# A piece of background work moved between the maxima and the sums of values in each attention step

## The chip, the cores and the metric

The kernel runs on one core of a Trainium2 chip. The metric is the device time of one execution, in microseconds (us); lower is better.

## The reference, cut to what matters

Two transformer layers with cross-attention act on x (2048 rows of 256 numbers, 16 heads of 16). Layer one splits x into two halves of 1024 rows: self-attention within each half, attention of each half to the other one, and an MLP with GELU. Layer two does self-attention under a mask that is given as integers (2048 x 2048), attention to a context of 1601 rows, and an MLP with ReLU.

```python
# layer one: x0, x1 are the two halves of x
x0 = x0 + g_msa[:, 0] * mha(mod(ln(x0)));  x1 = x1 + g_msa[:, 1] * mha(mod(ln(x1)))   # stage 0
ox = attend(qx, ky, vy) @ crs_proj_w;      oy = attend(qy, kx, vx) @ crs_proj_w       # stage 1
x  = x + g_mca * (ox, oy);  x = x + g_mlp * (gelu(z @ fc1 + b) @ fc2 + b)
# layer two
x = layernorm(x + mha(x, x, x, mask))          # stage 2, scores = where(mask == 0, -1e9, scores)
x = layernorm(x + mha(x, memory, memory))      # stage 3, memory: 1601 rows
x = layernorm(x + relu(x @ w1 + b1) @ w2 + b2)
```

## The kernel before, in words

The four attentions are four stages (0 to 3), and all of them run in one stream (`stream`). A **unit** is one block of 512 queries with one group of four heads. There are 16 units in each of the stages 0, 1 and 3, and 20 in stage 2, where one block's keys are taken in two parts. A unit has 16 steps in stages 0 and 1, 16 or 32 in stage 2, and 26 in stage 3: 1440 steps in all. A **step** handles one tile of 128 keys for two of the four heads. Stage 2 is the one with a mask (`masked`).

Each step puts up to four kinds of work on TensorE:

- **Scores** (`weights_of`, `second[s2]()` in `stream`): two matmuls at L938 and two at L945, which use 64 rows of the array each, so that two run side by side. With a mask two more at L953 add the bias, with the full 128 rows and 128 columns, in bf16. The result lies in a tile `s_ps` of two banks, and ScalarE's exponential (L958) takes it from there into `e`.
- **Maxima** of a later unit (`take_maxima`, L860), of the same 64-row shape, also into `s_ps`. VectorE reduces them, at L875, or at L868 with a mask. There are three tiles `s_ps`, and scores and maxima take them in turn. `todo` says at which step each is due. When all of a unit's maxima are there, VectorE negates and splits them (L885 to L891), and three steps later `as_rows` turns them into rows (L899); ScalarE copies these to `nm` (L904), which L945 of the next unit reads.
- **Sums of values** (`values_of`, L975): four matmuls side by side, each on 32 columns of the array. They run in two passes, so the trace has eight. They read `e` of tiles that are two steps old or older. Most steps have half a tile, 256 columns; the first and the last tile of a unit are taken whole, with an empty step after each.
- **Pieces** of background work: the projections, transposes and MLPs that turn the output of a stage into the input of the next. They are generators (`chain_self`, `chain_cross` and so on), and each of their matmul groups is a `piece`. A piece takes a PSUM bank, runs its matmuls, and yields; its last step is the **eviction**, which reads the bank. Lines: transposes L343 (eviction on ScalarE, L354 or L358), queries and keys L385 (ScalarE `hi` L392, then VectorE `lo` L393, then two stores), values L415 (VectorE L425), output projection L460 and the second half of the MLP L535 (VectorE L478 or L490), the first half of the MLP L515 (ScalarE L523). All matmuls of pieces use the full array and fp32, which runs in two passes.

While the stream runs, pieces use one of two single banks, `small[0]`. The other one holds the sums of values of the running unit, and the two change places after a unit's third step (`s2 == 2`). There ScalarE also copies the sums of the unit before out of its bank (`copy_sums`, L1007).

The order of instructions on every engine is the order in which the program issues them. In `stream` a step calls, in turn: `before()`, which evicts the piece of the step before; `take_maxima`; the sums of values and the scores (with a mask the scores first); and `after(step)`, which advances the counter `now`, does what is due in `later` (`as_rows`, reciprocals and divisions among it), makes mask columns (L828), issues one transfer (`load_ready`), and starts the next piece through `advance`. So the matmuls of a piece come after a step's last TensorE work, and its eviction comes first in the next step.

The MLP with GELU has a peculiarity: with `wait` set, its first half only adds the bias, and eight GELU activations (L534) run together in the first step of its second half (`down`), so that ScalarE's function table is changed once for the eight.

Of the kernel before, what the change touches and what calls it, by code (L numbers as in the profile page):

```python
# [66 lines left out]
def slot_rows(st, slot):  # L67
    return sum(key_rows(st, n) for n in KEYS[st][slot])


def slots_of(st, b):

    return ((b // 2,), (1 - b // 2,), (0, 1), (0, 1))[st]
# [3 lines left out]
def two_layers(ctx: ExitStack, tc: tile.TileContext, a: dict, out: bass.AP):  # L77
# [17 lines left out]

    small = [1]
    streaming = [False]
    unfinished: list = []

    def flush(banks):  # L100
# [93 lines left out]
    def hidden(shape, dtype=F32, name="hid"):  # L194
        return sb.tile(shape, dtype, tag="hidden", bufs=HB, name=name)
# [310 lines left out]
    def mlp(w, ci, func, hT, finish, between=None):  # L506
        w1, w2 = w
        hid: list = [None] * (DFF // P)


        wait = func != AF.Relu and streaming[0]

        def up(m, f):
            for k in range(2):
                nc.tensor.matmul(  # L515
                    m, lhsT=w1[k][:, f * P : (f + 1) * P], rhs=hT[:, k, :],
                    start=k == 0, stop=k == 1,
                )

        def take(m, f):  # L520
            hid[f] = hidden([P, BLK])
            bias = cols[:, ci + f : ci + f + 1]
            nc.scalar.activation(hid[f], m, AF.Identity if wait else func, bias=bias)  # L523

        for f in range(DFF // P):
            yield from piece(lambda m, f=f: up(m, f), lambda m, f=f: take(m, f))
        if between is not None:
            between()

        def down(m, n, q2):  # L530
            qt = 2 * n + q2
            for f in range(DFF // P):
                if wait and qt == 0:
                    nc.scalar.activation(hid[f], hid[f], func)  # L534
                nc.tensor.matmul(  # L535
                    m[:, q2 * D : (q2 + 1) * D], lhsT=hid[f][:, qt * P : (qt + 1) * P],
                    rhs=w2[f // 4][:, f % 4, :], start=f == 0, stop=f == DFF // P - 1,
                )

        for n in range(2):  # L540
            yield from piece(
                *(lambda m, n=n, q2=q2: down(m, n, q2) for q2 in range(2)),
                lambda m, n=n: finish(n, m.rearrange("p (t d) -> p t d", d=D)),
            )
# [555 lines left out]
    def stream(stages):  # L1100

        units = []
        for st in stages:
            for b in ORDER[st]:
                blocks[st, b] = {}
                if (st, b) == (2, SPLIT):
                    units += [
                        {"st": st, "b": b, "g": g, "slots": (slot,), "part": slot}
                        for slot in range(2) for g in range(NG)
                    ]  # L1110
                else:
                    units += [
                        {"st": st, "b": b, "g": g, "slots": slots_of(st, b)} for g in range(NG)
                    ]
        for i, u in enumerate(units):
            u["i"] = i

        columns: list = []
        at = 0
        for u in units:  # L1120
            steps = [(slot, kt) for slot in u["slots"] for kt in range(-(-slot_rows(u["st"], slot) // P))]
            if u["st"] == 2 and u["g"] == 0:
                columns += [
                    (at + 2 * n - COLUMNS, u["b"], slot, kt) for n, (slot, kt) in enumerate(steps)
                ]
            u["start"], u["steps"] = at, 2 * len(steps)
            at += 2 * len(steps)

        todo: list = []
        for u, w in zip(reversed(units), [*reversed(units[:-1]), None]):  # L1130
            tiles = maxima(u)
            n = len(tiles)
            begin, length = (w["start"], w["steps"]) if w else (-n, n)
            for k in range(n - 1, -1, -1):
                due = begin + k * length / n - AHEAD
                if u.get("part") == 1 and u["g"] == 0:

                    due = begin + (n - 1) * length / n - AHEAD - (n - 1 - k) * SPACING
                todo.append([min(due, todo[-1][0] - SPACING) if todo else due, u, tiles[k]])

        def take_maxima(step):
            while todo and todo[-1][0] <= step:
                _, u, f = todo.pop()
                f()
                if not todo or todo[-1][1] is not u:
                    all_maxima(u)

        def all_maxima(u):
            negated(u)
            later.append([3, lambda: as_rows(u), True])  # L1150
            if u.get("part") == 0 and u["g"] == NG - 1:
                want(2, 1, 1)

        def before():

            if unfinished and background and not background[0][2] and background[0][1] <= now[0]:
                if not advance(background[0]):
                    background.pop(0)

        def after(step):  # L1160

            now[0] += 1
            due = [x for x in later if x[0] <= 0]
            later[:] = [[x[0] - 1, *x[1:]] for x in later if x[0] > 0]
            for x in due:
                x[1]()
            turned = any(x[2] for x in due)
            while columns and columns[0][0] <= step:
                mask_columns(*columns.pop(0)[1:])
                turned = True  # L1170
            load_ready()
            soon = any(x[0] <= 0 and x[2] for x in later)
            soon = soon or (columns and columns[0][0] <= step + 1)
            if background and background[0][1] <= now[0]:
                if not background[0][2] or not (turned or soon):
                    if not advance(background[0]):
                        background.pop(0)

        streaming[0] = True
        for u in units[:2]:  # L1180
            load_queries(u)
        for step in range(math.floor(todo[-1][0]), 0):
            small[0] = 1
            before()
            take_maxima(step)
            after(step)
        pending: list = []
        step = 0
        for u in units:
            i = u["i"]  # L1190
            masked = u["st"] == 2
            small[0] = i % 2
            second = weights_of(u)
            for s2 in range(len(second)):
                before()
                if s2 == 3:
                    pending += values_of(u)
                if s2 == 1 and i + 2 < len(units):
                    load_queries(units[i + 2])
                take_maxima(step)  # L1200
                f = pending.pop(0) if pending else None
                if f and not masked:
                    f()
                second[s2]()

                if f and masked:
                    f()
                after(step)
                step += 1
                if s2 == 2:  # L1210
                    small[0] = (i + 1) % 2
                if s2 == 2 and i:
                    w = units[i - 1]
                    copy_sums(w)
                    part = w.get("part")
                    if part is None:
                        later.append([3, lambda w=w: invert(w), False])
                        later.append([6, lambda w=w: divide(w), False])
                    elif part == 1:
                        v = units[i - 1 - NG]  # L1220
                        later.append([3, lambda w=w, v=v: compare(w, v), False])
                        later.append([4, lambda w=w, v=v: invert_both(w, v), False])
                        later.append([7, lambda w=w: (fetch_first(w), divide(w)), False])
                    if w["g"] == NG - 1 and part != 0:
                        chain_after(w)
        small[0] = len(units) % 2
        for f in pending:
            if f:
                f()
        for x in later:  # L1230
            x[1]()
        flush((0, 1))
        streaming[0] = False
        w = units[-1]
        copy_sums(w)
        invert(w)
        divide(w)
        chain_after(w)
        while background:
            if not advance(background[0]):  # L1240
                background.pop(0)
        flush((None,))
# [92 lines left out]
```

## Time and profile before

| | us |
|---|---|
| median of 3 runs | 3392.64 |
| lowest and highest of them | 3391.25 and 3396.46 |
| profiled execution, its own time | 3403.53 |
| its span, first to last instruction | 3401.7 |
| TensorE matmuls busy | 3113.2 |
| VectorE busy | 2120.7 |
| ScalarE busy | 1713.7 |
| GpSimd busy | 404.6 |

The profiled execution has a time of its own, a little above the median. Numbers per instruction come from that one execution. The granted TensorE clock in it was 0.968 of full speed. From the first scores to the last, the four stages take 500, 639, 1237 and 815 us of the span; 131 us lie ahead of them and 79 us behind, counted from the start of one step's scores to that of another's.

In a line of the timeline the columns are the start, the duration, the engine, the line of the program, the operation, what it writes and reads, the shapes, and the number of instructions that are merged in the line; in square brackets stands the idle time ahead of it and what ended it. The ends of matmuls are modelled, so the distance between starts is the better measure on TensorE.

### The profile page before, as it was taken

The page shows a single profiled execution, that of the slowest core. Times are in us where ns is not written, and L with a number is a line of the kernel's source. Part 1 is how long each engine was busy: PE and PEld are TensorE (multiplying, and loading weights), DVE is VectorE, ACT ScalarE, POOL GpSimd, SP SyncE. Part 2 cuts the span into 40 slices and gives each one's busy share as a digit, 9 for nine tenths or more (in the row PEclk, how much of TensorE's full clock was granted, in tenths as well). Part 3 has the DMA queues.
Part 4 walks back from the last instruction along what each step waited for, and adds up shares of the span by engine and source line. Part 5 has one row for each costly group of instructions (what it writes and reads, how often), then busy time and mean ns, then how long its engine had stood idle before and what let it go on. Part 6 is the DMA issues. An engine that isn't in the chain of part 4 may idle for free.

```text
span 3401.7 us, 56761 instructions
## 1 busy us (share of the span) xinstructions
PE 3113.2 (92%) x22592; PEld 1362.0 (40%) x22592; DVE 2120.7 (62%) x3858; ACT 1713.7 (50%) x1868; POOL 404.6 (12%) x344
## 2 busy tenths in 40 slices
PE   4799999998999889898999999999999999999995
PEld 2334444444444433333333333343334444444433
DVE  2676766764646455366767777767656747657541
ACT  1265655655545445343555555554546646546461
POOL 0001101101010121104023012201010011110102
PEclk8799999999999999899999999999999999999997
DMA  5652162160204121343111001102241100000000
GB/s 177 140 105 65 36 117 65 48 128 24 65 18 114 32 84 37 94 100 107 51 39 51 15 20 58 32 17 55 49 87 43 26 10 26 25 18 26 10 14 16
DMA packets 162362, 191.20 MB, mean 56 GB/s; under 512 B 82584, under 2 KB 95520, under 8 KB 162096
## 3 DMA queue, kind: packets, MB, share of 16 engines
q1 hardware_dynamic: 162096, 187.57, 22.3%
q8 instruction: 178, 2.92, 0.4%
q14 instruction: 88, 0.72, 0.1%
HBM read 129.91 MB, written 48.46 MB: 52 GB/s over the span
## 4 chain that ended last, share of the span: by engine, by line
PE 51%; DVE 5%; ACT 4%; DMA 2%; SPq 2%; POOL 1%; issue 1%; ACTq 0%; POOLq 0%; DVEq 0%
PE m_ps L975 13%; PE s_ps L938 8%; PE s_ps L860 8%; PE s_ps L953 7%; PE s_ps L945 6%; ACT e L958 3%; PE m_ps L515 2%; DVE s_ps L868 2%; PE m_ps L535 2%; DVE pm L875 1%; PE m_ps L460 1%; DMA raw<-in_mask 1%; PE m_ps L385 1%; DVE t L328 1%; PE m_ps L415 1%
## 5 line engine op out<-in xcount | busy, mean ns | idle before, releaser
L958 ACT ACTIVATE e<-s_ps 128x1024 f32<-128x1024 f32 (+1 forms) x1440 | 1468.1, 1025 | 1375.0 <-PE s_ps L945 794.8
L875 DVE TENSOR_REDUCE pm<-s_ps 128x2 f32<-128x1024 f32 (+3 forms) x1024 | 1120.9, 1106 | 534.7 <-PE s_ps L860 530.2
L975 PE MATMUL m_ps<-e,V 128*32 128x256 f32 (+2 forms) x10432 | 903.6, 418 | 7.3 <-ACT hT L354 4.4
L868 DVE CUSTOM_DVE_ANT_0 s_ps<-s_ps,bias 128x512 f32<-128x512 f32 x1024 | 712.8, 701 | 295.4 <-PE s_ps L860 161.6
L860 PE MATMUL s_ps<-kT,q 64*128 64x512 f32 (+3 forms) x3072 | 676.6, 443 | 111.8 <-ACT e L958 51.1
L938 PE MATMUL s_ps<-q,kT 64*128 64x512 f32 (+1 forms) x2880 | 677.3, 466 | 51.8 <-ACT e L958 28.4
L945 PE MATMUL s_ps<-nm,sel 64*128 64x512 f32 (+1 forms) x2880 | 575.2, 395 | 0.1
L860 PEld LDWEIGHTS s_ps<-kT,q 64*128 64x128 f32 x3072 | 294.1, 186 | 528.1 <-issue 301.1
L938 PEld LDWEIGHTS s_ps<-q,kT 64*128 64x128 f32 (+1 forms) x2880 | 270.5, 184 | 496.6 <-issue 241.0
L975 PEld LDWEIGHTS m_ps<-e,V 128*32 128x32 f32 (+1 forms) x10432 | 206.9, 108 | 433.6 <-issue 415.3
L953 PE MATMUL s_ps<-biasT,ident 128*128 128x512 bf16 x1024 | 311.4, 386 | 0.0
L1053 POOL TENSOR_TENSOR oT<-oT,rd_rows 64x512 f32<-64x512 f32 x64 | 81.7, 1277 | 1904.8 <-DMA rd_rows<-rd_dr 1491.1
L945 PEld LDWEIGHTS s_ps<-nm,sel 64*128 64x128 f32 (+1 forms) x2880 | 275.2, 187 | 12.1 <-ACT nm L904 0.8
L805 POOL TENSOR_SCALAR bias<-raw 128x512 bf16<-128x512 int32 x64 | 123.1, 1924 | 266.4 <-DMA raw<-in_mask 256.4
L868 DVE DVE_READ_ACCUMULATOR2_ANT pm<- 128x1 f32 x1024 | 144.9, 141 | 0.0
L953 PEld LDWEIGHTS <-ident 128*128 128x128 bf16 x1024 | 58.4, 97 | 187.8 <-issue 187.8
L393 DVE SCALAR_TENSOR_TENSOR lo<-m_ps,qkb,hi 128x512 fp32r<-128x512 f32 (+2 forms) x56 | 41.1, 734 | 137.3 <-ACT hi L392 94.3
L535 PE MATMUL m_ps<-w_mlp,hid 128*128 128x256 f32 x448 | 111.4, 405 | 11.9 <-ACT hid L534 11.9
L385 PE MATMUL m_ps<-hT,w_qk 128*128 128x512 f32 (+2 forms) x224 | 109.8, 613 | 9.3 <-DVE lo L393 8.8
L515 PE MATMUL m_ps<-hT,w_mlp 128*128 128x512 f32 x224 | 111.0, 618 | 1.1 <-ACT hT L354 1.1
L535 PEld LDWEIGHTS m_ps<-w_mlp,hid 128*128 128x128 f32 x448 | 86.3, 200 | 36.5 <-ACT hid L534 16.3
L415 PE MATMUL m_ps<-w_v,hT 128*128 128x256 f32 (+1 forms) x212 | 58.0, 420 | 21.8 <-DVE lo L393 21.4
(106 smaller groups left out, 1220.9 us busy)
## 6 DMA issues: line engine op xcount, KB each, us to landing
q<-q_dr SPq DMA_DIRECT2D x544, 64.0 KB
kT<-k_dr SPq DMA_DIRECT2D x192, 128.0 KB
raw<-in_mask SPq DMA_DIRECT2D x64, 256.0 KB
q_dr<-hi SPq DMA_DIRECT2D x32, 256.0 KB
q_dr<-lo SPq DMA_DIRECT2D x32, 256.0 KB
oT<-sums SPq DMA_DIRECT2D x256, 32.0 KB
rd_rows<-rd_dr SPq DMA_DIRECT2D x64, 128.0 KB
v_dr<-v SPq DMA_DIRECT2D x14, 544.0 KB
```

Source lines behind the costliest of these rows:

```text
L385: nc.tensor.matmul(m[:, :n], lhsT=wqk[:, k, w, c, :], rhs=hT[:, k, :n], start=k == 0, stop=k == 1)
L515: nc.tensor.matmul(m, lhsT=w1[k][:, f * P : (f + 1) * P], rhs=hT[:, k, :], start=k == 0, stop=k == 1,)
L535: nc.tensor.matmul(m[:, q2 * D : (q2 + 1) * D], lhsT=hid[f][:, qt * P : (qt + 1) * P], rhs=w2[f // 4][:, f % 4, :], start=f == 0, stop=f = ...
L805: nc.gpsimd.tensor_scalar(bias_rows[b, slot, qt][:, j * BLK : (j + 1) * BLK], raw, 0.0, MASKED, ALU.is_equal, ALU.mult,)
L860: nc.tensor.matmul(s[:, h, :nn], lhsT=u["q"][64 * h : 64 * h + 64, i, qt * P : (qt + 1) * P], rhs=kT[g][slot][64 * h : 64 * h + 64, i, c : ...
L868: nc.vector.tensor_tensor_reduce(out=s[:, h, :], in0=s[:, h, :], in1=bias_rows[b, slot, qt][:, c : c + nn], scale=1.0, scalar=-3.0e38, op0 ...
L875: nc.vector.tensor_reduce(u["pm"][:, qt, :, i, n], s[:, :, :nn], AX.X, ALU.max)
L938: nc.tensor.matmul(s[:r, h, :], lhsT=kT[g][slot][64 * h : 64 * h + 64, i, kt * P : kt * P + r], rhs=u["q"][64 * h : 64 * h + 64, i, :], st ...
L945: nc.tensor.matmul(s[:r, h, :], lhsT=sel[64 * h : 64 * h + 64, i, :r], rhs=u["nm"][64 * h : 64 * h + 64, :], start=False, stop=not masked,)
L953: nc.tensor.matmul(s[:, h, :], lhsT=ident16, rhs=bias_columns[b, slot, kt], start=False, stop=True,)
L958: nc.scalar.activation(e[:r], s[:r], AF.Exp, scale=SCALE)
L975: nc.tensor.matmul(u["av"][PH * j : PH * (j + 1), cut], lhsT=V[g][slot][:r, kt * GW + j * VW : kt * GW + j * VW + PH], rhs=u["e"][n, j % 2 ...
```

## The change

In steps without a mask the piece and all else of `after(step)` are issued between the maxima and the sums of values, and the piece's eviction, now called `evict`, comes in the same step, ahead of the scores and their exponential. In steps with a mask the scores come first as before, then `after(step)` and the piece, and then the sums of values; the eviction stays at the start of the next step. The flag `behind` is set by the MLP with GELU when its second half begins and cleared in that half's first step; in the step in which it is found set, `after(step)` is called last, as before.

```diff
+    behind = [False]
...
         def down(m, n, q2):
             qt = 2 * n + q2
+            behind[0] = False
             for f in range(DFF // P):
...
+        behind[0] = wait
         for n in range(2):
             yield from piece(
...
-        def before():
+        def evict():
...
             for s2 in range(len(second)):
-                before()
+                if masked:
+                    evict()
                 if s2 == 3:
                     pending += values_of(u)
                 if s2 == 1 and i + 2 < len(units):
                     load_queries(units[i + 2])
                 take_maxima(step)
                 f = pending.pop(0) if pending else None
-                if f and not masked:
+                if masked:
+                    second[s2]()
+                late = behind[0]
+                if not late:
+                    after(step)
+                if f:
                     f()
-                second[s2]()
-
-                if f and masked:
-                    f()
-                after(step)
+                if not masked:
+                    evict()
+                    second[s2]()
+                if late:
+                    after(step)
                 step += 1
```

More of the change, by code (lines that the diff above doesn't have):

```diff
@@ L1194, in stream @@
             for s2 in range(len(second)):
-                before()
+                if masked:
+                    evict()
                 if s2 == 3:
@@ L1201, in stream @@
                 f = pending.pop(0) if pending else None
-                if f and not masked:
-                    f()
-                second[s2]()
-                if f and masked:
-                    f()
-                after(step)
+                if masked:
[4 more added lines that the diff above has]
+                if f:
+                    f()
+                if not masked:
+                    evict()
+                    second[s2]()
+                if late:
+                    after(step)
                 step += 1
```

## The prediction

> **What bounds the kernel now.** I read the head of the page, then the chain that ended last, then TensorE's timeline step by step.
>
> ```profile
> PE 3113.2 (92%) x22592; PEld 1362.0 (40%) x22592; DVE 2120.7 (62%) x3858; ACT 1713.7 (50%) x1868; POOL 404.6 (12%) x344
> PE 51%; DVE 5%; ACT 4%; DMA 2%; SPq 2%; POOL 1%; issue 1%; ACTq 0%; POOLq 0%; DVEq 0%
> ```
>
> TensorE is busy 92% of the span and has most of the chain; nothing else comes near. So the question is what a step costs on TensorE. I call its groups M (maxima, L860), V (sums of values, L975), S (scores, L938 and L945, with a mask also L953), X (a piece), N (negated maxima as rows, L899), T (mask columns, L828). A plain unmasked step, columns start, duration, instruction:
>
> ```profile
> 256.60 0.51 PE L938 MATMUL s_ps<-q,kT 64*128 64x512 f32 x2
> 256.94 0.40 PE L945 MATMUL s_ps<-nm,sel 64*128 64x512 f32 x2
> 257.16 0.41 PE L860 MATMUL s_ps<-kT,q 64*128 64x512 f32 x2
> 257.51 0.64 PE L975 MATMUL m_ps<-e,V 128*32 128x256 f32 x8
> 258.07 0.50 PE L938 MATMUL s_ps<-q,kT 64*128 64x512 f32 x2
> ```
>
> From S to S it takes 1.47 us. Only starts are used here, as ends are modelled. With a piece:
>
> ```profile
> 823.45 0.50 PE L938 MATMUL s_ps<-q,kT 64*128 64x512 f32 x2
> 823.78 0.40 PE L945 MATMUL s_ps<-nm,sel 64*128 64x512 f32 x2
> 824.11 1.98 PE L515 MATMUL m_ps<-hT,w_mlp 128*128 128x512 f32 x4
> 826.03 0.51 PE L860 MATMUL s_ps<-kT,q 64*128 64x512 f32 x2
> 826.46 0.64 PE L975 MATMUL m_ps<-e,V 128*32 128x256 f32 x8
> 827.03 0.50 PE L938 MATMUL s_ps<-q,kT 64*128 64x512 f32 x2
> ```
>
> It takes 3.58 us with no wait, so the piece adds 2.11, though from its start to M's is only 1.92. Three sizes explain it. A **change of tile shape** costs 0.09: L945 to L860 (same shape) is 0.22, L945 to the piece 0.33. A **first 64-row pair after another shape** costs 0.11 more: L938 to L945 is 0.34 after V, 0.24 after M (1343.72 below). The piece's first matmul takes 0.53 to the next, later ones 0.43. With a mask:
>
> ```profile
> 1321.53 0.61 PE L953 MATMUL s_ps<-biasT,ident 128*128 128x512 bf16 x2
> 1321.98 1.88 PE L515 MATMUL m_ps<-hT,w_mlp 128*128 128x512 f32 x4
> 1323.79 0.50 PE L860 MATMUL s_ps<-kT,q 64*128 64x512 f32 x2
> ...
> 1343.72 0.40 PE L938 MATMUL s_ps<-q,kT 64*128 64x512 f32 x2
> 1343.96 0.40 PE L945 MATMUL s_ps<-nm,sel 64*128 64x512 f32 x2
> 1344.29 0.60 PE L953 MATMUL s_ps<-biasT,ident 128*128 128x512 bf16 x2
> 1344.82 0.64 PE L975 MATMUL m_ps<-e,V 128*32 128x256 f32 x8
> 1345.39 1.98 PE L515 MATMUL m_ps<-hT,w_mlp 128*128 128x512 f32 x4
> 1347.31 0.50 PE L860 MATMUL s_ps<-kT,q 64*128 64x512 f32 x2
> ```
>
> The masked S ends in L953, whose shape is the piece's own. Straight after it (at 1321.98, a step without V) the piece takes 1.81 to M instead of 1.92, and L953 to the piece is 0.45 where L953 to V is 0.53. ScalarE beside the unmasked piece above:
>
> ```profile
> 824.28 1.02 ACT L958 ACTIVATE e<-s_ps 128x1024 f32<-128x1024 f32 x1 [1.04 <-PE s_ps L945]
> 826.13 0.69 ACT L523 ACTIVATE hid<-m_ps,cols 128x512 f32<-128x512 f32 x1 [0.82 <-PE m_ps L515]
> 827.86 1.02 ACT L958 ACTIVATE e<-s_ps 128x1024 f32<-128x1024 f32 x1 [1.04 <-PE s_ps L945]
> ```
>
> The exponential starts 0.83 after its S, the eviction 0.63 after the piece's last matmul (825.50). ScalarE idles before both.
>
> **What the Trainium skill says.** "TensorEngine Tiling (Array Packing)", Key Properties, says that changing the tiling mode drains the engine. It gives no price; the trace has 0.09 us, also between 128x128 and 128x32. "TensorE: Matmul & The Clock Gate", The mechanism, says that a weight load overlaps running matmuls only where the row groups differ; that fits the dearer first pair after V, but the trace doesn't prove it. The table at the head of that page calls ScalarE's queue a strict FIFO; in the lines above eviction and exponential run one after the other, in program order.
>
> **The change part by part.** It adds and removes no instruction. On SP, POOL and VectorE the order stays: transfers, a piece's stores, the next query loads, and likewise reductions and evictions, follow each other as before. Two queues change. TensorE's unmasked order goes from M V S X to M X V S, its masked one from M S V X to M S X V; N and T move with X. On ScalarE, without a mask, the copy of N and a piece's eviction go ahead of the same step's exponential. Masked steps keep ScalarE's order.
>
> 1. *Unmasked, with a V in the step.* New step: S 0.34 and 0.22 (M follows in the same shape), M 0.35, X 1.91, V 0.57, together 3.38 against 3.58: **0.20** less, one change of shape and one first pair. N: 2.25 now (254.35 to 256.60), then 1.47 and its own 0.59, 0.19 less. Going through the trace's matmuls in order I count 152 X, 47 N and 3 T: 202 x 0.20 = **40 us**. The 22 unmasked X in steps without V save nothing.
> 2. *Masked, with V.* V 0.57, M 0.34, L938 0.24, L945 0.33, L953 0.45, X 1.81: 3.74 against 3.92. There are 60 X, 20 N and 51 T; 131 changes of shape x 0.093 = 12.2, first matmul 0.105 cheaper on 45 wide X = 4.7, 0.055 on 15 transposes and 20 N = 1.9: **19 us**.
> 3. *Projections of queries and keys.* Here the next X waits in the same bank for hi (0.69, ScalarE) and then lo (0.75, VectorE). Lo ends 2.10 after X's last matmul begins, the next X starts at 2.18: just in time. The new distance is 0.52 + 0.57 + 0.56 + 0.32 = 1.97, so it waits 0.2. 30 unmasked pairs: **-6 us**. Evictions in one operation end near 1.38 and have room.
> 4. *The bank of the sums.* After the third step of a unit ScalarE copies the last unit's sums (L1007, 0.59) and the next X takes that bank. Now X follows M at once. S to exponential 0.83, exponential 1.02, copy 0.59: free 2.45 after S. X could start at 0.89, or at 1.43 without a piece in the third step (M waits for an exponential there now). 14 unmasked units have an X in the fourth step, 7 of them after one in the third: 7 x 1.56 + 7 x 1.0 = 18 lost. Against it, V no longer waits for the third step's eviction (steps of 4.05 three times where 2.68 would do, and five others: 8 us), and X in the fifth step not for the fourth's (0.37 x 11 = 4). Net **-6 us**.
> 5. *Exponential behind the eviction.* Eviction ends 0.63 + 0.69 = 1.32 after X's last matmul begins; S begins at 0.52 + 0.57 = 1.09, its exponential at 1.92. Slack 0.60: cost nothing; the cover is V and S. Without it, up to 0.69 a piece. Bounded below: no gain either, since the exponential still waits for S.
> 6. *GELU blocks.* `behind` keeps 8 activations of 0.615 and the table loads (1.28) after the exponential, as now; three such steps lose the 0.2. About 15 further steps wait for a DMA or POOL today and can't use the gain. Together **-4 us**.
>
> Sum: 40 + 19 - 6 - 6 - 4 = **43 us**. The profiled execution took 3403.5 (span 3401.7), 11 above the median 3392.6; I take the 43 from both: 3360 there, **3349** as median. With items 3 and 4 at nought it is 55 less, with both doubled and a fifth of 1 and 2 not reached 19 less.
>
> **The rivals.**
> - *Only the shape change is saved.* If M behind S is no cheaper, and X behind L953 as dear as behind V, 333 x 0.093 = 31 remains, less 16: 15 us, 3378. Against it are the 0.24 and 1.81 above; for it that M straight before X is hardly seen in this trace.
> - *Not what it says.* TensorE might be held by ScalarE and VectorE in these steps, and move its idle time only: 3393. For it, exponentials hold M in 84 matmul waits (51 us); against it, the piece steps show none.
> - *Slower: evictions expose the exponential.* An eviction that comes over 0.60 late delays the exponential, over 0.8 also the M two steps on, which needs its bank. Late ones exist: of the hi, five start 1.1 to 4.0 after the last matmul. If all 174 unmasked pieces paid 0.69, 120 - 43 = 77 more: 3470. Some 60 paying in full would cancel the gain. Most evictions start at 0.63, so I give it little.
>
> **How the numbers follow.** A measurement tells 0.2%, 6.8 us, from no change. Forecast as worked out 0.68, its own range 3338 to 3374 by the ends above; only the shape change 0.20; not what it says 0.05; slower 0.07. Of the second, 0.19 is still faster by over 0.2%, and a little of it is not: faster 0.87, same 0.06, slower 0.07. The range 3332 to 3380 takes in the first two.
>
> **What would show it.** Timeline: an unmasked piece step M, X, V, S of 3.38, a masked one of 3.74; L860 after L945 at 0.22 everywhere; the exponential still 0.83 after S in piece steps. Waits: X on the copy of sums L1007, some 18 us in 14 places, absent now; L385 and L415 longer on lo. Wrong if M behind S costs over 0.3, if X to V is dearer than 0.52 after its last matmul, or if TensorE waits for L958 more than now.

## The result, and the profile after

| | before | changed |
|---|---|---|
| median, first comparison (6 runs each) | 3395.49 us | 3372.09 us |
| ratio changed to before, 95% interval | | 0.9923 (0.9905 to 0.9941) |
| the same in a second comparison | | 0.9918 (0.9894 to 0.9942) |
| span of the profiled execution | 3401.7 us | 3366.3 us |

The change makes the kernel 0.8% faster: 26 to 28 us by the two ratios, where 43 were forecast. (The medians of the table are 23 us apart; the intervals of the two ratios allow 20 to 36.) The profiled pair lies 35 us apart, at a granted TensorE clock of 0.968 before and 0.967 after. The head of the changed kernel's page, and the engines' shares of its chain:

```profile
PE 3061.2 (91%) x22592; PEld 1374.3 (41%) x22592; DVE 2129.0 (63%) x3858; ACT 1712.1 (51%) x1868; POOL 404.7 (12%) x344
PE 52%; DVE 5%; ACT 4%; DMA 2%; POOL 1%; SPq 1%; issue 1%; ACTq 0%; POOLq 0%; DVEq 0%
```

The same instructions run, and TensorE is still the bound. Its busy time is 52 us shorter, but the span only 35: its idle time grew from 289 to 305 us. The lines of the program have moved by one to three: maxima M are L863, scores S L941, L948 and L956, sums of values V L978, the exponential L961, the MLP piece X L516. TensorE's timeline of an unmasked piece step:

```profile
809.30 0.50 PE L941 MATMUL s_ps<-q,kT 64*128 64x512 f32 x2
809.64 0.40 PE L948 MATMUL s_ps<-nm,sel 64*128 64x512 f32 x2
809.86 0.40 PE L863 MATMUL s_ps<-kT,q 64*128 64x512 f32 x2
810.20 1.99 PE L516 MATMUL m_ps<-hT,w_mlp 128*128 128x512 f32 x4
812.11 0.64 PE L978 MATMUL m_ps<-e,V 128*32 128x256 f32 x8
812.68 0.50 PE L941 MATMUL s_ps<-q,kT 64*128 64x512 f32 x2
```

From S to S it is 3.38 us instead of 3.58. M follows S after 0.22, in the same tile shape, and the piece takes its 1.91 to V. With a mask:

```profile
1320.39 1.88 PE L516 MATMUL m_ps<-hT,w_mlp 128*128 128x512 f32 x4
1322.20 0.64 PE L978 MATMUL m_ps<-e,V 128*32 128x256 f32 x8
1322.77 0.50 PE L863 MATMUL s_ps<-kT,q 64*128 64x512 f32 x2
1323.10 0.39 PE L941 MATMUL s_ps<-q,kT 64*128 64x512 f32 x2
1323.33 0.40 PE L948 MATMUL s_ps<-nm,sel 64*128 64x512 f32 x2
1323.66 0.61 PE L956 MATMUL s_ps<-biasT,ident 128*128 128x512 bf16 x2
1324.10 1.88 PE L516 MATMUL m_ps<-hT,w_mlp 128*128 128x512 f32 x4
```

From piece to piece it is 3.71 instead of 3.92. The piece stands straight behind L956, whose shape it has, and takes 1.81. ScalarE beside the first of these two stretches:

```profile
810.14 1.02 ACT L961 ACTIVATE e<-s_ps 128x1024 f32<-128x1024 f32 x1 [0.61 <-PE s_ps L948]
812.22 0.69 ACT L524 ACTIVATE hid<-m_ps,cols 128x512 f32<-128x512 f32 x1 [1.06 <-PE m_ps L516]
813.52 1.02 ACT L961 ACTIVATE e<-s_ps 128x1024 f32<-128x1024 f32 x1 [0.61 <-PE s_ps L948]
```

The eviction ends at 812.91, and the exponential waits 0.61 longer, for its scores. What stands against the gain is in TensorE's own waits (total in us, times, longest), in the changed kernel:

```profile
PE s_ps L863 <- ACT e L961: 60.0, 93, 1.2
...
PE s_ps L941 <- ACT e L961: 25.1, 82, 0.7
...
PE m_ps L344 <- ACT sums L1010: 12.9, 10, 1.4
...
PE m_ps L386 <- DVE lo L394: 12.1, 15, 1.7
...
PE m_ps L516 <- ACT sums L1010: 4.3, 3, 1.4
```

and the same waits before:

```profile
PE s_ps L860 <- ACT e L958: 51.1, 84, 1.2
...
PE s_ps L938 <- ACT e L958: 28.4, 94, 0.9
...
PE m_ps L385 <- DVE lo L393: 8.8, 8, 1.6
```

The waits on the copy of the sums are new, 17.2 us in 13 places. Those of query and key pieces on lo grew by 3, and those of the maxima on an exponential by 9.

I cut both traces at the starts of S and sorted the stretches by whether either trace has a piece, negated maxima or mask columns there (the work that was moved), or none of them (plain). Differences to before in us; the second profiled execution of the same kernel is beside the first.

| | first | second |
|---|---|---|
| stretches with moved work, unmasked stages 0, 1, 3 | -19.0 | -31.6 |
| the same, masked stage 2 | -18.4 | -11.2 |
| plain stretches, stage 3 | +10.2 | +9.9 |
| plain stretches, stages 0 to 2 | -3.8 | -0.1 |
| ahead of the first scores | -3.9 | -3.4 |

So the stretches that the change touches give 37 and 43 us, and plain steps of stage 3, in which no instruction was moved, take 10 back in both. Two executions of one kernel differ by 13 and 7 us in the first two rows, so only their sum can be read.

### The profile page after: what moved, and what is told of

The parts are those of the page before. It is cut to its first block, busy times and chain, and to the rows that moved or that the text cites. A ratio compares the mean times of both kernels' runs of the same rounds, so it can differ in the third digit from the quotient of the medians.

```text
span 3366.3 us, 56775 instructions
## 1 busy us (share of the span) xinstructions
PE 3061.2 (91%) x22592; PEld 1374.3 (41%) x22592; DVE 2129.0 (63%) x3858; ACT 1712.1 (51%) x1868; POOL 404.7 (12%) x344
## 4 chain that ended last, share of the span: by engine, by line
PE 52%; DVE 5%; ACT 4%; DMA 2%; POOL 1%; SPq 1%; issue 1%; ACTq 0%; POOLq 0%; DVEq 0%
PE m_ps L978 14%; PE s_ps L941 9%; PE s_ps L863 8%; PE s_ps L956 7%; PE s_ps L948 6%; ACT e L961 3%; PE m_ps L516 2%; DVE s_ps L871 2%; PE m_ps L537 2%; PE m_ps L461 1%; DVE pm L878 1%; DMA raw<-in_mask 1%; PE m_ps L386 1%; DVE t L329 1%; POOL bias L808 1%
## 5 line engine op out<-in xcount | busy, mean ns | idle before, releaser
L961 ACT ACTIVATE e<-s_ps 128x1024 f32<-128x1024 f32 (+1 forms) x1440 | 1468.4, 1025 | 1333.9 <-PE s_ps L948 739.6
L978 PE MATMUL m_ps<-e,V 128*32 128x256 f32 (+2 forms) x10432 | 907.5, 419 | 1.0 <-DVE lo L394 0.8
L863 PE MATMUL s_ps<-kT,q 64*128 64x512 f32 (+3 forms) x3072 | 655.9, 428 | 120.3 <-ACT e L961 60.0
L941 PE MATMUL s_ps<-q,kT 64*128 64x512 f32 (+1 forms) x2880 | 679.8, 468 | 44.2 <-ACT e L961 25.1
L948 PE MATMUL s_ps<-nm,sel 64*128 64x512 f32 (+1 forms) x2880 | 575.8, 395 | 0.0
L863 PEld LDWEIGHTS s_ps<-kT,q 64*128 64x128 f32 x3072 | 295.3, 187 | 488.7 <-issue 255.6
L941 PEld LDWEIGHTS s_ps<-q,kT 64*128 64x128 f32 (+1 forms) x2880 | 270.5, 184 | 501.7 <-issue 283.0
L978 PEld LDWEIGHTS m_ps<-e,V 128*32 128x32 f32 (+1 forms) x10432 | 207.0, 108 | 442.3 <-issue 421.9
L956 PE MATMUL s_ps<-biasT,ident 128*128 128x512 bf16 x1024 | 311.4, 386 | 0.0
L948 PEld LDWEIGHTS s_ps<-nm,sel 64*128 64x128 f32 (+1 forms) x2880 | 275.4, 187 | 10.6 <-ACT nm L907 0.5
L956 PEld LDWEIGHTS <-ident 128*128 128x128 bf16 x1024 | 58.3, 97 | 187.5 <-issue 187.5
L537 PE MATMUL m_ps<-w_mlp,hid 128*128 128x256 f32 x448 | 111.6, 405 | 11.9 <-ACT hid L536 11.9
L386 PE MATMUL m_ps<-hT,w_qk 128*128 128x512 f32 (+2 forms) x224 | 108.9, 609 | 13.8 <-DVE lo L394 12.1
L516 PE MATMUL m_ps<-hT,w_mlp 128*128 128x512 f32 x224 | 110.3, 615 | 4.3 <-ACT sums L1010 4.3
L393 ACT ACTIVATE hi<-m_ps,qkb 128x512 fp32r<-128x512 f32 (+2 forms) x56 | 37.8, 675 | 75.1 <-PE m_ps L386 58.3
```

The lines of the kernel that those rows point to most:

```text
L386: nc.tensor.matmul(m[:, :n], lhsT=wqk[:, k, w, c, :], rhs=hT[:, k, :n], start=k == 0, stop=k == 1)
L516: nc.tensor.matmul(m, lhsT=w1[k][:, f * P : (f + 1) * P], rhs=hT[:, k, :], start=k == 0, stop=k == 1,)
L537: nc.tensor.matmul(m[:, q2 * D : (q2 + 1) * D], lhsT=hid[f][:, qt * P : (qt + 1) * P], rhs=w2[f // 4][:, f % 4, :], start=f == 0, stop=f = ...
L863: nc.tensor.matmul(s[:, h, :nn], lhsT=u["q"][64 * h : 64 * h + 64, i, qt * P : (qt + 1) * P], rhs=kT[g][slot][64 * h : 64 * h + 64, i, c : ...
L941: nc.tensor.matmul(s[:r, h, :], lhsT=kT[g][slot][64 * h : 64 * h + 64, i, kt * P : kt * P + r], rhs=u["q"][64 * h : 64 * h + 64, i, :], st ...
L948: nc.tensor.matmul(s[:r, h, :], lhsT=sel[64 * h : 64 * h + 64, i, :r], rhs=u["nm"][64 * h : 64 * h + 64, :], start=False, stop=not masked,)
```

## The experiments

All times are compared with the kernel before on the same chip. Where tiles are "in turn", the three tiles for scores and maxima have names of their own and are taken 1, 2, 3, 1 and so on. Otherwise the framework chooses one of three when the program is built. Its choice is not always the next in turn, as the description of the kernel before has it: in stage 0 of that program, 27 of the 256 scores get the tile of the scores just before them. e1 to e4 ran on one chip, e5 to e8 on a second and e9 and e10 on a third, so runs of different groups are compared by their ratios.

**Each half alone.** e1 keeps the masked order as it was, e2 the unmasked one.

```diff
 # e1, masked steps, against the change
 second[s2]()
-after(step)
 f()
+after(step)
```

```python
# e2, unmasked steps, cut to the order of the calls
evict()
take_maxima(step)
f()
second[s2]()
after(step)
```

> The new order in the steps without a mask alone; masked steps keep scores, sums of values, piece. Theory (a change of tile shape and a first 64-row pair saved, 0.20 us for each of 202 unmasked steps, less the waits on lo and on the copy of the sums and what the choice of the score tiles does): unmasked piece steps of 3.38 us, masked ones still 3.92, about 13 to 17 us faster than before, 3380. Rival (the gain comes from the masked steps alone, the unmasked order is neutral or worse, since eviction now delays the exponential): 0 or slower than before. Rival (everything comes from the score tiles): the change of this run lies in plain steps without a piece.

Measured: 3380.57 against 3396.81, ratio 0.9957 (0.9939 to 0.9975). Typical steps with L516 are 3.38 unmasked and still 3.92 masked.

> The new order in the masked steps alone; unmasked steps as before. Theory: 131 masked steps with V save one change of shape each, wide pieces also a dearer first matmul: masked piece steps 3.72, steps with mask columns 2.25, unmasked piece steps still 3.58; stage 2 some 19 us shorter, in all 3374 or 19 less than before. Rival (only idle time moves): no difference from before. If the two halves add up, this and the unmasked half give the 23 to 26 us of the full change between them.

Measured: 3382.33, ratio 0.9955 (0.9939 to 0.9971). Such steps are 3.57 unmasked and 3.72 masked. Each half is worth some 15 us and they add up to what the whole brings; the gain is neither that of one half nor idle time moved. Plain stretches do not carry e1's gain: in stage 3 they lose 14.5 us in its trace, and in e2's they are unchanged (-0.2). The maxima's waits on an exponential are 60.0 us in 93 places in e1, as in the change, and 51.0 in 84 in e2, as before. What disturbs stage 3 comes with the unmasked order.

**The choice of the score tiles.**

```diff
-return ps.tile([P, 2, BLK], dtype, tag="s", bufs=3, name="s_ps")
+turn[0] = (turn[0] + 1) % 3
+return ps.tile([P, 2, BLK], dtype, tag=f"s{turn[0]}", bufs=1, name="s_ps")
```

> The kernel before, with the three score tiles taken strictly in turn instead of by the choice of the program's framework (1, 2, 3, 1, ...). Theory: where the choice departs from turns, scores or maxima wait for an exponential that has just begun; with turns those waits in plain steps go (S behind the exponential 37 us, M 66 us now, part of them), 20 to 40 us faster than before. Rival: TensorE is ahead of ScalarE in those stretches anyway and the wait only moves to another instruction: within 7 us of before.

Measured: 3389.3, ratio 0.9977 (0.9967 to 0.9988), 8 us: close to the rival's 7, and far from the 20 of the theory. The waits of maxima and scores on exponentials fell by 39 us (51.1 to 32.9, and 28.4 to 7.9), but their waits on VectorE's reductions rose by 31 (the scores' with L868 as releaser from 11.8 to 21.8, with L875 from 8.7 to 25.3, the maxima's with L875 from 18.7 to 22.8). Most of it only moves.

> The changed kernel with the three score tiles strictly in turn. Theory: the changed order alters which tile the framework chooses, and 10 us of the expected gain were lost so in plain steps of stage 3; with turns in both, the difference between this and the kernel before with turns is the order alone: 33 to 40 us, more than the 23 to 26 between the two without turns. Rival: the choice of tiles is chance and costs both alike; then the difference stays at 23 to 26.

Measured: 3357.23, ratio 0.9883 (0.9862 to 0.9904). Against e3 that is 0.0094 or 32 us, short of the 33 expected and above the rival's 26, and the intervals are too wide to part them. The traces say more. Against e3 the stretches with moved work are 40 us shorter in e4, and the plain ones of stage 3 are 4 longer instead of 10. One step of stage 3 before, in the change, and in the change with tiles in turn (M is L860, L863, L866), each without a piece:

```profile
2669.99 0.53 PE L860 MATMUL s_ps<-kT,q 64*128 64x352 f32 x4
2670.44 0.64 PE L975 MATMUL m_ps<-e,V 128*32 128x256 f32 x8
2671.33 0.50 PE L938 MATMUL s_ps<-q,kT 64*128 64x512 f32 x2 [0.24 <-ACT e L958]
```

```profile
2630.64 0.32 PE L863 MATMUL s_ps<-kT,q 64*128 64x352 f32 x2
2631.98 0.47 PE L863 MATMUL s_ps<-kT,q 64*128 64x448 f32 x2 [1.02 <-ACT e L961]
2632.39 0.64 PE L978 MATMUL m_ps<-e,V 128*32 128x256 f32 x8
2632.95 0.67 PE L941 MATMUL s_ps<-q,kT 64*128 64x512 f32 x2
```

```profile
2630.78 0.54 PE L866 MATMUL s_ps<-kT,q 64*128 64x352 f32 x4
2631.24 0.64 PE L981 MATMUL m_ps<-e,V 128*32 128x256 f32 x8
2632.12 0.50 PE L944 MATMUL s_ps<-q,kT 64*128 64x512 f32 x2 [0.24 <-ACT e L964]
```

Two pairs of maxima stand in this step. Before, the second follows at once (four in one line). In the change it waits 1.02 for an exponential that has just begun, although nothing of this step was moved. In the built program this second pair has the tile of the scores just before, with only one pair of maxima in between; ten pairs of stage 3 have got such a tile, where the program before has none. Both traces of the change have ten waits of 0.98 to 1.02 us of maxima in stage 3, the trace before has none of that length, and with turns they are gone. In plain steps of stage 3 the maxima's waits on an exponential add up to 13.7 us before and 22.7 in the change, but to 11.3 in both e3 and e4. So the tiles cause these 9 us of waits; the scores' waits on an exponential are 1.5 shorter there, and what the other 2 or 3 of the 10 us are is not shown.

**The fourth step and the copy of the sums,** both with tiles in turn.

```diff
 # e5
-late = behind[0]
+late = behind[0] or (not masked and s2 == 3)
 # e8
-if s2 == 2 and i:
+if s2 == 1 and i:
     w = units[i - 1]
     copy_sums(w)
```

> The changed kernel with tiles in turn, and in the fourth step of an unmasked unit the piece stands behind the scores again, so that it comes after the copy of the sums. Theory (the 14 pieces of those steps wait some 18 us for the copy of the sums): that wait goes from the trace, 14 shape changes come back (14 x 0.20 = 3); 8 to 15 us faster than the changed kernel with turns. Rival (ScalarE is behind there in any case and the wait moves to the maxima or to the sums of values): within 5 us of it.

Measured: 3348.9, ratio 0.9859 (0.9836 to 0.9882), 8 us below e4 by the ratios, with overlapping intervals. So neither its theory nor its rival (within 5 us) is settled by the times.

> The changed kernel with tiles in turn, and the copy of the sums one step earlier, after a unit's second step, where its last sums are done. Theory: the bank is free when the fourth step's piece comes, the 18 us of waits on that copy go and no shape change comes back; the third step's exponential starts 0.6 later, which its readers don't see; 10 to 18 us faster than the changed kernel with turns. Rival (the copy ahead of the third step's exponential holds up the maxima two steps on, in all 67 units): slower, up to 0.6 x 47 = 28 us.

Measured: 3355.42, ratio 0.9877 (0.9853 to 0.9901): no gain on e4 that can be told, where 10 to 18 us were expected. Its rival falls too: the maxima's waits on exponentials are 33.9 us, in e4 32.7. TensorE's waits in e8:

```profile
PE m_ps L419 <- DVE lo L397: 31.5, 6, 13.8
...
PE m_ps L389 <- DVE lo L397: 18.0, 17, 1.9
```

In both the waits on the copy of the sums have left the trace, as expected. But in e4 these two lines were 16.9 and 11.7 us, so in e8 the value and the query and key projections wait 21 us more for lo; in e5 it is 9 more (25.7 and 11.4). The value projections' part is 17 to 21 us in the other traces (25 in e7), so most of e8's rise is beyond that scatter and much of e5's is not. What delays lo is in the traces too, first e4, then e8:

```profile
DVE lo L397 <- DMA k_dr<-hi: 23.8, 5, 8.7
```

```profile
DVE lo L397 <- DMA k_dr<-hi: 40.2, 5, 15.3
```

Lo itself waits for a store of an earlier hi. The longest of these waits stands ahead of the longest wait of the value projection, 13.8 us in e8 and 7.3 in e4. That fits a chain of pieces which starts sooner and only reaches its next wait sooner. Whether earlier stores would save this time was not tried.

**Eviction last, and the piece behind the sums of values,** with tiles in turn.

```diff
 # e7, steps without a mask
-evict()
 second[s2]()
+evict()
 # e6, steps without a mask
 take_maxima(step)
+f()
 after(step)
-f()
 evict()
 second[s2]()
```

> The changed kernel with tiles in turn, but without a mask the eviction stands behind the step's exponential on ScalarE. Theory: an eviction can then begin only when the exponential has ended, some 2.3 us later than now, and the next piece waits for its bank, about 1.7 us for each of some 110 pieces that follow another: 150 to 200 us slower than the changed kernel with turns. Rival (evictions ahead delay the exponentials and so TensorE): faster.

Measured: 3590.07, ratio 1.0567 (1.0540 to 1.0594), 233 us slower than e4, more than the 150 to 200 expected. ScalarE and TensorE in one piece step:

```profile
914.24 1.02 ACT L964 ACTIVATE e<-s_ps 128x1024 f32<-128x1024 f32 x1 [3.37 <-PE s_ps L951]
915.16 0.68 ACT L527 ACTIVATE hid<-m_ps,cols 128x512 f32<-128x512 f32 x1
```

```profile
913.97 0.39 PE L866 MATMUL s_ps<-kT,q 64*128 64x512 f32 x2
915.89 1.98 PE L519 MATMUL m_ps<-hT,w_mlp 128*128 128x512 f32 x4 [1.53 <-ACT hid L527]
```

The matmuls of the last piece were done long before, but its eviction stands behind the exponential, and the next piece waits 1.53 for it. A step with an MLP piece takes 4.97 us; the median step with queries or keys, which need hi and then lo, takes 7.30 instead of 3.60. The maxima's waits on exponentials are 32.5 us, as in e4 (32.7), so an eviction ahead does not hold up TensorE through the exponential. With the piece in this place, the eviction must stand ahead of the exponential.

> The changed kernel with tiles in turn, but without a mask the piece stands behind the sums of values, straight ahead of the scores: maxima, sums of values, piece, scores. Theory: as many changes of shape and first pairs, so piece steps of 3.38 us as well; the fourth step's piece waits about 1.0 less for the copy of the sums; one-operation evictions end 1.32 after the piece's last matmul and the exponential could begin at 1.35: just covered. Same to 10 us faster than the changed kernel with turns. Rival (eviction ahead of the exponential is dear once its cover, the sums of values, is gone): exponentials start over 0.83 after their scores and maxima wait for them; slower by 20 us or more.

Measured: 3339.07, ratio 0.9830 (0.9805 to 0.9856), 18 us below e4 by the ratios, more than expected. Piece steps are 3.38 here too, with a different neighbour on either side. The waits on the copy of the sums fell from 17.2 to 4.4 us, which is most of the gain; the rest is not accounted for. ScalarE's work in e6:

```profile
807.05 0.69 ACT L527 ACTIVATE hid<-m_ps,cols 128x512 f32<-128x512 f32 x1 [1.63 <-PE m_ps L519]
807.78 1.02 ACT L964 ACTIVATE e<-s_ps 128x1024 f32<-128x1024 f32 x1
```

Eviction and exponential stand back to back with no idle time, and the exponential starts 0.84 after its S (806.94), as in any plain step. The slack was there to be used, to the last hundredth.

> The change with the framework's own choice of score tiles, but without a mask the order maxima, sums of values, piece, scores. Theory: what the order gained with turns in both (0.983 against 0.9883, mostly waits on the copy of the sums) it gains here too: 0.986 to 0.989, and the waits on the copy of the sums are under 5 us. Rival (the gain came with the turns): no faster than the change.

Measured: 3354.68 against 3397.72, ratio 0.9869 (0.9846 to 0.9892), 16 us below the change on the same chip (3370.28, last experiment) and with an interval just below its own; the waits on the copy of the sums are 4.4 us. So the gain does not hang on the turns.

**The change once more.**

> The change itself once more, in more rounds. The two halves alone gave 0.9957 and 0.9955; if they add up, and the median is what the change is worth, 0.991 to 0.993. Rival (the profiled pair, 35 us apart, is the better estimate and the first medians were chance): 0.989 to 0.990.

Measured: 3370.28, ratio 0.9918 (0.9894 to 0.9942), as expected, though the interval reaches the rival's 0.990. The medians stand; the profiled pair overstates the gain, since the profiled execution before lies 8 us above the median of 3395.49 and the changed one 4 below its own.

## Why the prediction was right or wrong

The range and the direction were right, and so were the mechanism of the gain and most of its terms. The central figure, 43 us, was 15 to 17 us too large.

- **Items 1 and 2, the tile shapes: right, in the size of a step too.** 3.38 against 3.38 unmasked, 3.71 against 3.74 masked, 2.06 against 2.06 with negated maxima. e1 and e2 show both halves, and e6, with a different order and as few changes of shape, has the same 3.38. The rival of only the shape change would need 3.49 unmasked, and falls. The passage on weight loads and row groups that the prediction puts beside the dearer first pair does not explain it, as the last section shows.
- **Item 3, lo: right.** The wait of L386 on lo rose from 8.8 to 12.1 us, that of its weight loads not counted; 20 of the 32 unmasked steps with a query or key piece and sums of values stayed at 3.55 to 3.68 and gained nothing, as expected.
- **Item 4, the bank of the sums: right in its parts.** 17.2 us were measured for the 18, up to 1.42 each. On the other side, the sums of values waited 7.0 us for evictions before (hT 4.7, lo 1.2, hid 1.1) and 0.8 after, where 8 were forecast. That removing the 17.2 would give about as much back was a later expectation: it failed in e8 and is not settled in e5. e6 keeps what it saves.
- **Item 5, the exponential: right.** It idles 0.61 where 0.60 of slack were worked out, and e6 uses that slack up. The slower rival falls: no waits of its kind appear in the piece steps, and what makes the kernel slower is e7's opposite order.
- **Item 6, the GELU blocks:** the wait for the eight activations is 11.9 us in 4 places before and after. The rest of this term was not measured by itself.
- **One sign of being wrong came true by its letter.** TensorE waits for the exponential more than before: maxima and scores together 85.1 us instead of 79.5. The growth comes from the ten waits in plain steps of stage 3, not from exponentials that evictions delayed.
- **Where the size failed.** The sum took plain steps as untouched. The step that failed is "It adds and removes no instruction", with the count "Two queues change": a third thing changed, the choice of the tiles for scores and maxima when the program is built. Plain steps of stage 3 took 10 us longer in both profiled executions; 9 us of new waits of the maxima, gone with the tiles in turn, are most of it. The touched stretches themselves gave 37 and 43 us where 43 were forecast; that the second meets the forecast is in part luck, as the first shows.
- **What stays open.** The plain and touched stretches of the two profiles together give 31 and 33 us, the ratios 26 to 28, and their intervals reach 32 and 36. The 3 to 4 us ahead of the first scores are not the change's: the first scores start at 131.0 us in the profile before, at 125.6 and 126.7 in e3 and e2, which keep the old unmasked order, at 127.1 and 127.6 in the change, and at 131.4 in e6. Runs of one kernel spread by 3 to 27 us here, and no profile exists of a run near the median of before, so the remaining 4 or 5 us cannot be placed.

e6 is the best version measured: the order maxima, sums of values, piece, scores without a mask, with the score tiles in turn, 1.7% faster than before.

## What to carry to other kernels

On a TensorE-bound kernel with small matmuls of several tile shapes, count the changes of shape in a step and order the groups so that equal shapes meet; starts of consecutive matmuls price a change to the hundredth of a microsecond. Then ask of the moved group what frees its bank and what its eviction delays, and put it where that slack is. When a program's buffers are chosen by a framework, look again at the steps that were not moved. And before removing a wait, look what the work behind it will wait for next.

## What the runs showed of the hardware that I had not expected

The changes among the three shapes 64x128, 128x128 and 128x32 that the traces can price all cost 0.09 us. In the profiles before and after, the next matmul starts 0.216 us after a 256-column fp32 pass of the full array if it has the same shape, and 0.309 after it if it has 64x128 or 128x32; after a 64x128 pair the figures are 0.23 and 0.32 (medians). From 128x32 there is nothing of the same shape to compare with, as its four matmuls run side by side; to either other shape it is 0.309. It made no difference which came first: the piece between maxima and sums, or between sums and scores, took 3.38 us a step.

The traces also show that weights are not loaded ahead across such a change. TensorE's weight loads before, beside the piece at 824.11 that the prediction shows:

```profile
823.56 0.19 PEld L945 LDWEIGHTS s_ps<-nm,sel 64*128 64x128 f32 x2
824.11 0.30 PEld L515 LDWEIGHTS m_ps<-hT,w_mlp 128*128 128x128 f32 x2 [0.36 <-issue]
824.65 0.19 PEld L515 LDWEIGHTS m_ps<-hT,w_mlp 128*128 128x128 f32 x1 [0.24 <-issue]
825.08 0.19 PEld L515 LDWEIGHTS m_ps<-hT,w_mlp 128*128 128x128 f32 x1 [0.24 <-issue]
```

The piece's first load starts with its matmul, at 824.11; the other three start while the matmul before their own runs (the second is merged with the first in this view). In the whole profile before, the load at each of some 3,700 changes among the three shapes starts within 0.03 us of its matmul, while 2,391 of 2,414 full-array matmuls that follow one of their own shape have their load earlier, 0.21 us in the median. The sentence of the Trainium skill that the prediction cites, by which a weight load overlaps running matmuls only where the row groups differ, does not hold here: L945's load at 823.56 runs beside L938's matmuls, which began at 823.45, on the same rows. A load that is not hidden fits the dearer first pair after another shape and the piece's dearer first matmul (0.53 instead of 0.43), but no run tests it.
